# Second cross-attention: queries six places ahead, turned rows and the second half's inverse one place sooner, the last output product behind a feed-forward

## The chip, the cores and the metric

The kernel runs on one core of one Trainium2 chip. A core has a matrix engine (TensorE, PE in the profile), a vector engine (VectorE, DVE), a scalar engine (ScalarE, ACT), a general engine (GpSimd, POOL) and a queue that issues most of the DMA transfers (SyncE, SP). The metric is the device time of one execution in microseconds (us). All data are 32-bit floats.

## The reference, cut to what matters

The reference computes two transformer blocks on x of shape (8, 512, 256): eight images of 512 rows. Each block has self-attention, cross-attention to a short context and a feed-forward. The change lies in the second block's cross-attention and in the start of its feed-forward:

```python
cross_in = _adaln(x, cond, ln1_w, ln1_b, g1_w, g1_b, b1_w, b1_b)
ctx_n = _ln(context, ca_lnc_w, ca_lnc_b)
x = _attn(cross_in, ctx_n, ca_wq, ca_wkv, ca_wo, ca_bo) + x   # 16 heads of 64, 64 context rows
ffn_in = _adaln(x, cond, ln2_w, ln2_b, g2_w, g2_b, b2_w, b2_b)
h = jax.nn.gelu(ffn_in @ ff_w1 + ff_b1, approximate=False)
x = h @ ff_w2 + ff_b2 + x
```

`_attn` projects queries, keys and values, rotates queries and keys by position (rope), takes the softmax of their products and multiplies the result with the values and with `wo`.

## The kernel before

The kernel is one program of stages. The first block's stages and the second block's self-attention take up to about 1829 us of the profile. Then `cross()` does the second cross-attention of all eight images, and after it `feed_forward()` does the second feed-forward, image by image. In these stages the instructions of TensorE, VectorE, ScalarE and GpSimd run in the order in which the Python code issues them (a manual schedule). The order of SP's DMA queue is chosen by a planner, which may move a transfer ahead of another that is not ready by its own estimate. [...]

`cross()` runs a loop of eight places j = 0 to 7 for each image b. An image has 8 pairs of heads, and one place issues one query projection. The pieces are these.

- `queries(n)` projects one eighth of an image's queries (two matmuls of 128x512, recorded as four), and VectorE multiplies the result with the cosines and sines (L853, L854). Two successive n form one group: after the odd one, GpSimd makes the two turned query tiles by a subtraction and an addition (L858, L859). It runs LEAD places ahead, into eight query buffers; the products lie in five `t` buffers.
- `turn(b)` transposes the normalised rows of image b on TensorE (L429), and ScalarE evacuates them with scale and shift (L430) into `hT`, which the queries read.
- `score(b, half)` multiplies the queries of half the heads with the keys; ScalarE takes the exponentials (L1280) into `p`.
- `sums(b, half)` sums `p` over the context on TensorE. ScalarE copies the sums into the single `den` buffer (L1290), two DMAs write them to DRAM (L1293), and one DMA reads them back spread over 128 partitions into `rec` (L1295).
- `inverse(b, half)` takes the reciprocal of `rec` on VectorE (L1300), writes it to DRAM (L1302), and eight DMAs read it back, spread over partitions, into the four `rb` buffers (L1307).
- `scaled(b, half)` multiplies the four 512-column pieces of `p` of that half with `rb`, by turns on GpSimd and VectorE (L1314).
- `outer(b, pp)` multiplies the values of the context with the output weights, once for each image, into `vw` (evacuated by ScalarE, L1251).
- `cross_out(b, t)` makes output tile t: eight matmuls over all pieces of `p`, the first half's four ahead of the second half's, added to x by VectorE (L466).
- `rows_(i, n)` is one of three pieces of the layer norm of a later image (VectorE, and GpSimd for the root and for adding a bias row); `load_kb` and `load_vb` load the next images' keys and values (L963, L968).

Four PSUM banks go round among all users of `bank_x()`. A bank is taken again at the fourth call after it and must have been evacuated by then. The scores have two double banks of their own.

In a place the order is: sums, scores, turn, queries, outer, scaled, inverse, cross_out, loads, rows. An image's second half is only worked off in the next image's places: `sums(b-1, 1)` in place 0, `inverse(b-1, 1)` in place 2, `scaled(b-1, 1)` in place 4, `cross_out(b-1, ...)` in places 5, 6 and 7. For the first half they are `sums(b, 0)` in place 4, `inverse(b, 0)` in place 6 and `scaled(b, 0)` in place 0 of the next image.

`feed_forward()` issues for each image four `up` steps (matmuls into the score banks, Gelu on ScalarE, L1342), a `turn` for the next image, and four `down` steps (matmuls, addition to x, store to the output, L1350). In image 0 the last cross-attention's remaining steps lie between: the last `scaled`, `inverse` and `scaled` after the `up` steps 0, 1 and 2, and the last `cross_out` of four tiles.

Of the kernel before, what the change touches and what calls it, by code (L numbers as in the profile page):

```python
# [17 lines left out]
B, N, D, H, T, CD, FF = 8, 512, 256, 16, 64, 192, 1024  # L18
# [69 lines left out]
def fast_path(ctx: ExitStack, tc: tile.TileContext, a: dict, out: bass.AP):  # L88
# [56 lines left out]
    def row(name):  # L145
        lo, hi = _ROWS[name]
        return rows[:, lo:hi]
# [285 lines left out]
    def normed_in_pieces(pool, b, eps, take):  # L433

        def rows_():
            z = pool.tile([P, NT, D], F32, tag="z", name="z", bufs=1)
            take(z)
            return z

        return norm_pieces(rows_, xs[b], eps)  # L440
# [7 lines left out]
    def add_row(b, r):  # L448

        nc.gpsimd.tensor_tensor(xs[b], xs[b], r[:, None, :].to_broadcast([P, NT, D]), ALU.add)  # L450
# [511 lines left out]
    def load_kb(b):  # L962
        nc.sync.dma_start(kvs[b % 2][0], k_d[:, :, :, b, :].rearrange("p g e t -> p (g e) t"))  # L963

    def load_vb(b):
        for e in range(2):
            r = slice(64 * e, 64 * e + 64)
            nc.sync.dma_start(kvs[b % 2][1][r, :, e, :], v_d[r, :, b, :])  # L968
# [13 lines left out]
    with tc.tile_pool(name="ph4", bufs=2) as wk:  # L982
# [160 lines left out]
        for b, (score, value, sums, inverse, scaled, out_tiles, _) in enumerate(todo):  # L1143
            base = 2 * NG * b
            for g in range(NG):
                if b == B - 1 and g == NG - 1:
                    break
                n = base + 2 * g + 2
# [65 lines left out]
    with tc.tile_pool(name="ph5", bufs=2) as wk:  # L1214
# [9 lines left out]
        def rows_(i, n=None):  # L1224

            if i < 2 * B:
                b = i % B
                if not n and i not in pieces:
                    pieces[i] = normed_in_pieces(nk, b, EPS1, lambda z: turned_rows.update({i: z}))
                for piece in pieces[i] if n is None else pieces[i][n : n + 1]:  # L1230
                    piece()
                if n in (None, 2):
                    add_row(b, row("ffb2" if i // B else "cabo"))

        def turn(i):
            if i < 2 * B:
                am, bm = ((a1, b1), (a2, b2))[i // B]
                turned_rows[i] = transposed((nk, wk)[i % 2], turned_rows[i], i % B, am, bm, 1)
# [3 lines left out]
        def outer(b, pp):  # L1242

            s = ss[b]
            if pp == 0:
                s["vw"] = wk.tile([P, NPAIR, D], F32, tag="vw", name="vw")
            ps = bank_x()
            for i in range(2):
                p = 2 * pp + i
                mm(ps[:, i * D : (i + 1) * D], kvs[b % 2][1][:, p, :, :].rearrange("p e k -> p (e k)"), w_co[:, p, :])  # L1250
            nc.scalar.copy(s["vw"][:, 2 * pp : 2 * pp + 2, :], ps.rearrange("p (i d) -> p i d", i=2))  # L1251

        def queries(n):
            b, m = divmod(n, NPAIR)
            if b == B:
                return
            g, e = divmod(m, 2)
            ps = bank_x()
            for k in range(2):
                mm(ps, w_cq[:, k, m * P : (m + 1) * P], turned_rows[b][:, k, :], k == 0, k == 1)  # L1260

            def dst():
                ss[b][g] = [wk.tile([P, N], F32, tag="q", name="q", bufs=8) for _ in range(2)]
                return ss[b][g]

            rope_half(wk, ss[b], g, e, ps[:, None, :], rope_c[:, None, :], rope_s[:, None, :], [P, 1, N], 5, dst)

        def score(b, half):
            s = ss[b]
            pss = [bank_s() for _ in range(2)]  # L1270
            for e in range(2):
                for j in range(4):
                    r = slice(32 * j, 32 * j + 32)
                    for i in range(2):
                        g = 2 * half + i
                        mm(pss[j // 2][64 * i : 64 * i + 64, j % 2, :], kvs[b % 2][0][r, 2 * g + e, :], s[g][e][r, :],
                           e == 0, e == 1)
            for u in range(2):
                s["p", 2 * half + u] = pr = wk.tile([P, 2, N], F32, tag="p", name="p", bufs=8)
                nc.scalar.activation(pr, pss[u], AF.Exp, scale=HD1 ** -0.5)  # L1280

        def sums(b, half):

            s = ss[b]
            d = bank_x()
            for j in range(4):
                p = 4 * half + j
                mm(d[32 * j : 32 * j + 32, :], sel0, s["p", p // 2][:, p % 2, :])
            den = wk.tile([P, N], F32, tag="den", name="den", bufs=1)
            nc.scalar.copy(den, d)  # L1290
            dd = dram.tile([4, 2, N], F32, tag="den5", name="den5")
            for e in range(2):
                nc.sync.dma_start(dd[:, e, :], den.rearrange("(j r) n -> j r n", j=4)[:, e, :])  # L1293
            s["rec", half] = rec = wk.tile([P, 8 * N // P], F32, tag="rec", name="rec")
            nc.sync.dma_start(rec, flat(dd))  # L1295
# [13 lines left out]
        def scaled(b, half):  # L1309
            s = ss[b]  # L1310
            for j in range(4):
                p = 4 * half + j
                pr = s["p", p // 2][:, p % 2, :]
                (nc.gpsimd, nc.vector)[p % 2].tensor_tensor(pr, pr, s["rb", j], ALU.mult)  # L1314

        def out_tile(b, t, lhsT, w):
            s = ss[b]

            if t % 2 == 0 or b == B - 1 and w is w_f2 and t > 1:
                s["ps"] = bank_x()  # L1320
            project_tile(s["ps"], t % 2, lhsT, w, 8, t)
            if b == B - 1 and w is w_f2 and t > 1:
                x = xs[b][:, t, :]
                nc.vector.tensor_tensor(x, s["ps"][:, (t % 2) * D : (t % 2 + 1) * D], x, ALU.add)
            elif t % 2:
                add_to(b)(t // 2, s["ps"].rearrange("p (j d) -> p j d", j=2))

        def cross_out(b, t):
            out_tile(b, t, lambda k: ss[b]["p", k // 2][:, k % 2, :], ss[b]["vw"])
# [40 lines left out]
            return good  # L1370

        def cross():
            LEAD = 5
            for n in range(LEAD):
                queries(n)
                if n:
                    outer(0, n - 1)
            nc.gpsimd.memset(kvs[1][1], 0.0)
            for b in range(B):
                for j in range(NPAIR):  # L1380
                    if j == 0 and b:
                        sums(b - 1, 1)
                    if j == 4:
                        sums(b, 0)
                    if j % 4 == 0:
                        score(b, j // 4)
                    if j == 2:
                        turn(b + 1)
                    queries(NPAIR * b + j + LEAD)
                    if b and j < 2:  # L1390
                        for pp in (2 * j, 2 * j + 1):
                            outer(b, pp)
                    if b:
                        if j == 0:
                            scaled(b - 1, 0)
                        if j == 2:
                            inverse(b - 1, 1)
                        if j == 4:
                            scaled(b - 1, 1)
                        if j > 4:  # L1400
                            for t in ((0,), (1,), (2, 3))[j - 5]:
                                cross_out(b - 1, t)
                    if j == 2 and b + 1 < B:
                        load_kb(b + 1)
                        load_vb(b + 1)
                    if j > 4:
                        rows_(b + 2, j - 5)
                    if j == 6:
                        inverse(b, 0)
            sums(B - 1, 1)  # L1410

        def feed_forward():
            good = top = None
            for b in range(B):
                for ff in range(4):
                    up(b, ff)
                    if b == 0 and ff < 3:
                        (lambda: scaled(B - 1, 0), lambda: inverse(B - 1, 1), lambda: scaled(B - 1, 1))[ff]()
                if b == 0:
                    for t in range(4):  # L1420
                        cross_out(B - 1, t)
                turn(B + b + 1)
                for t in range(4):
                    down(b, t)
                    if t == 1:
                        rows_(B + b + 2)
                if b == 1:
                    top = extremes()
                if b == 2:
                    good = within(top)  # L1430
            return good

        with tc.manual_schedule(engines={ENG.PE, ENG.DVE, ENG.Activation, ENG.Pool}):
            cross()
            return feed_forward()
# [862 lines left out]
```

## Time and profile before

| What | us |
|---|---|
| Median of 3 runs (lowest to highest) | 2396.58 (2392.86 to 2398.16) |
| Profiled execution, its own time | 2397.98 |
| Its span, from the first to the last instruction | 2396.4 |
| Mean granted TensorE clock | 0.994 |
| First score of the second cross-attention starts | 1828.81 |
| Its images 1 to 7 start at | 1849.08, 1894.57, 1938.18, 1980.10, 2023.61, 2065.53, 2108.99 |
| Its last sums | 2148.56 |
| First `up` of the feed-forward | 2149.56 |

A line of the timeline has the start in us, the duration in us, the engine, the line of the kernel, the operation, what it writes and reads, and how many instructions it merges; in brackets stands the idle time ahead of it on its engine and what ended it. A matmul of 32-bit floats is recorded as two. SPq is the issue of a DMA on the SP queue, not the transfer. In a line of the windows come the window, its length, the busy time (and instructions) of PE, weight loads, DVE, ACT and POOL, then the granted TensorE clock, the DMA engines' busy share and GB/s.

### The profile page before, as it was taken

Reading aid. Unit: us, or ns where it says so; the run is one execution under the profiler, and the core shown is the slowest. Engines: PE = TensorE matmul, PEld = TensorE weight load, DVE = VectorE, ACT = ScalarE, POOL = GpSimd, SP = SyncE. Lnnn points to the kernel's source line nnn. Section 1 sums busy time; section 2 is a strip of 40 time slices with the busy share of each in tenths; the row PEclk is TensorE's granted clock in tenths of the full one; section 3 lists DMA queues with packets and bytes.
Section 4 is the critical chain, followed back from the end, with each engine's and each line's share of the span. In section 5 each row is a group of like instructions: output and inputs, shape, how many; then the busy total and the mean of one; then the engine's idle time right before and its main releaser. Section 6 shows DMA issues by size and latency. Waiting matters only on the chain.

```text
span 2396.4 us, 29139 instructions
## 1 busy us (share of the span) xinstructions
PE 2356.0 (98%) x11348; PEld 1146.4 (48%) x11348; DVE 1079.1 (45%) x2043; ACT 885.4 (37%) x1118; POOL 953.4 (40%) x582
## 2 busy tenths in 40 slices
PE   9999999999999999999999999999999999999998
PEld 4333544544545633434343434343445555557666
DVE  4454544544445345454545455554444444431110
ACT  4665545545542134243434333333342212111221
POOL 4563223323210046464645555555544444431110
PEclk9999999999999999999999999999999999999999
DMA  5120000000003000000101000000123212110000
GB/s 185 37 103 12 16 15 13 17 14 6 12 11 97 0 1 28 14 24 10 28 10 28 10 28 10 26 12 20 44 68 99 68 57 67 60 56 31 18 21 21
DMA packets 84307, 83.85 MB, mean 35 GB/s; under 512 B 42192, under 2 KB 59328, under 8 KB 84160
## 3 DMA queue, kind: packets, MB, share of 16 engines
q1 hardware_dynamic: 82680, 78.73, 10.9%
q8 instruction: 91, 1.49, 0.3%
q0 software_dynamic: 576, 2.10, 0.2%
q10 hardware_dynamic: 904, 1.07, 0.1%
q14 instruction: 56, 0.46, 0.1%
HBM read 71.83 MB, written 10.04 MB: 34 GB/s over the span
## 4 chain that ended last, share of the span: by engine, by line
PE 94%; issue 2%; POOL 1%; DMA 1%; DVE 1%; ACT 1%; SPq 1%; POOLq 0%; ACTq 0%; DVEq 0%
PE ps_X L118 39%; PE ps_S L118 23%; PE ps_D L118 16%; PE ps_O L118 14%; PE ps_X L429 1%; DMA rb<-rec 1%; POOL p L1314 1%; PE ps_X L616 1%; SPq L1307 0%; PE ps_X L576 0%; ACT p L596 0%; DMA rec<-rec 0%; PE ps_D L616 0%; POOL var L567 0%; PE ps_D L429 0%
## 5 line engine op out<-in xcount | busy, mean ns | idle before, releaser
L118 PE MATMUL ps_S<-q,k 32*128 32x512 f32 (+1 forms) x3072 | 416.4, 622 | 2.5 <-ACT p L596 1.5
L1037 ACT ACTIVATE p<-ps_S 128x1024 f32<-128x1024 f32 x256 | 248.4, 1021 | 449.5 <-PE ps_S L118 449.2
L596 ACT ACTIVATE p<-ps_S 128x1024 f32<-128x1024 f32 x256 | 248.2, 1022 | 197.7 <-PE ps_S L118 197.0
L1056 DVE TENSOR_TENSOR sm<-sm,p 128x1024 f32<-128x1024 f32 x128 | 251.4, 2022 | 0.2 <-ACT p L1037 0.2
L118 PEld LDWEIGHTS ps_S<-q,k 32*128 32x128 f32 (+1 forms) x3072 | 141.6, 183 | 228.0 <-issue 161.5
L1019 POOL TENSOR_TENSOR q<-t 128x512 f32<-128x512 f32 x32 | 59.7, 1866 | 328.1 <-DVE t L1017 287.0
L184 POOL TENSOR_TENSOR rstd<-rstd,mhalf 128x4 f32<-128x4 f32 x49 | 50.1, 1023 | 344.4 <-DVE rstd L183 343.8
L1016 DVE TENSOR_TENSOR t<-ps_X,rope_c 128x512 f32<-128x512 f32 x126 | 86.9, 690 | 211.9 <-PE ps_X L118 211.8
L567 POOL TENSOR_TENSOR var<-var,mhalf 128x32 f32<-128x32 f32 (+1 forms) x17 | 87.4, 5141 | 173.7 <-DVE var L561 170.3
L1052 POOL TENSOR_TENSOR sm<-p 128x1024 f32<-128x1024 f32 x64 | 150.0, 2370 | 1.9 <-ACT p L1037 1.9
L118 PE MATMUL ps_X<-hT,w 128*128 128x512 f32 x328 | 150.4, 597 | 0.0
L1102 POOL TENSOR_TENSOR oT<-oT,rb 128x512 f32<-128x512 f32 x63 | 125.2, 2007 | 30.5 <-DMA rb<-rec_d 26.6
L118 PE MATMUL ps_O<-p,v 128*64 128x512 f32 x512 | 134.9, 605 | 0.0
L118 PE MATMUL ps_D<-p,v 128*64 128x512 f32 x512 | 131.6, 592 | 0.0
L118 PE MATMUL ps_O<-p,h 128*32 128x512 f32 x1024 | 130.4, 610 | 0.8 <-ACT p L596 0.8
L118 PE MATMUL ps_X<-w_sa_wv,hT 128*128 128x512 f32 x256 | 118.3, 605 | 0.0
L118 PE MATMUL ps_X<-hT,w_sa_wq 128*128 128x512 f32 x256 | 115.9, 595 | 0.0
L118 PE MATMUL ps_X<-w_sa_wo,oT 128*128 128x256 f32 x512 | 113.9, 381 | 0.6 <-DVE t L1017 0.5
L118 PE MATMUL ps_X<-hT,w_sa_wk 128*128 128x512 f32 x248 | 113.2, 599 | 0.0
L118 PE MATMUL ps_S<-hT,w_ff_w 128*128 128x512 f32 x256 | 111.3, 593 | 0.0
L466 DVE TENSOR_TENSOR x<-ps_X,x 128x512 f32<-128x512 f32 x27 | 18.7, 691 | 198.1 <-PE ps_X L118 198.1
L118 PEld LDWEIGHTS ps_X<-w_sa_wo,oT 128*128 128x128 f32 x512 | 96.1, 190 | 22.8 <-issue 5.3
(282 smaller groups left out, 3543.3 us busy)
## 6 DMA issues: line engine op xcount, KB each, us to landing
rb<-rec SPq DMA_DIRECT2D x128, 128.0 KB
rb<-rec_d SPq DMA_DIRECT2D x124, 128.0 KB
rb<-rec SPq DMA_DIRECT2D x16, 256.0 KB
out_dram<-x SPq DMA_DIRECT2D x15, 256.0 KB
x<-in_x_dram SPq DMA_DIRECT2D x7, 512.0 KB
gate<-modd SPq DMA_DIRECT2D x24, 128.0 KB
k_d<-q POOLq DMA_DIRECT2D x4, 512.0 KB, 3.2
v_d<-v SPq DMA_DIRECT2D x8, 256.0 KB
```

The costliest lines, as they stand in the source:

```text
L118: nc.tensor.matmul(o, lhsT, rhs, start=start, stop=stop)
L184: nc.gpsimd.tensor_tensor(r[:, :n], r[:, :n], mhalf[:, :n], ALU.pow)
L429: nc.tensor.transpose(ps[:, t * P : (t + 1) * P], z[:, t, k * P : (k + 1) * P], ident)
L567: nc.gpsimd.tensor_tensor(var, var, half, ALU.pow)
L596: nc.scalar.activation(pr[u], pss[u], AF.Exp, scale=HD0 ** -0.5)
L616: nc.tensor.transpose(ps[:, t * P : (t + 1) * P], s["oT", g][:, t * P : (t + 1) * P], ident)
L1016: nc.vector.tensor_tensor(c, ps, rope_c, ALU.mult)
L1019: nc.gpsimd.tensor_tensor(r[0], ec, os, ALU.subtract)
L1037: nc.scalar.activation(pr, pss[u], AF.Exp, scale=HD1 ** -0.5)
L1052: nc.gpsimd.tensor_tensor(sm, s["p", g, 0, u], s["p", g, 1, u], ALU.add)
L1056: nc.vector.tensor_tensor(s["sm", g, u], s["sm", g, u], s["p", g, t, u], ALU.add)
L1102: eng.tensor_tensor(o, o, s["rb", g, u], ALU.mult)
```

## The change

The queries run six places ahead of the loop in place of five. The call of `turn` for the next image and the call of `inverse` for the previous image's second half move from place 2 to place 1. In the feed-forward, the last image's `cross_out` moves from ahead of `turn` and `down` of image 0 to behind them. The condition at `outer` keeps its four calls ahead of the loop.

```diff
         def cross():
-            LEAD = 5
+            LEAD = 6
             for n in range(LEAD):
                 queries(n)
-                if n:
+                if 0 < n < 5:
                     outer(0, n - 1)
...
                     if j % 4 == 0:
                         score(b, j // 4)
-                    if j == 2:
+                    if j == 1:
                         turn(b + 1)
                     queries(NPAIR * b + j + LEAD)
...
                         if j == 0:
                             scaled(b - 1, 0)
-                        if j == 2:
+                        if j == 1:
                             inverse(b - 1, 1)
                         if j == 4:
                             scaled(b - 1, 1)
...
                         (lambda: scaled(B - 1, 0), lambda: inverse(B - 1, 1), lambda: scaled(B - 1, 1))[ff]()
-                if b == 0:
-                    for t in range(4):
-                        cross_out(B - 1, t)
                 turn(B + b + 1)
                 for t in range(4):
                     down(b, t)
                     if t == 1:
                         rows_(B + b + 2)
+                if b == 0:
+                    for t in range(4):
+                        cross_out(B - 1, t)
```

## The prediction

> **What bounds the kernel now.** I read the page first: TensorE is busy nearly always, so only its gaps, and stretches where it runs slowly, can be won.
>
> ```profile
> PE 2356.0 (98%) x11348; PEld 1146.4 (48%) x11348; DVE 1079.1 (45%) x2043; ACT 885.4 (37%) x1118; POOL 953.4 (40%) x582
> ```
>
> Second, what TensorE waited for (us in total, times, longest). Five of the seventeen rows belong to the stage that changes:
>
> ```profile
> PE ps_O L118 <- POOL p L1314: 8.3, 6, 2.2
> PE ps_X L118 <- POOL p L1314: 7.8, 5, 2.2
> PE ps_D L118 <- POOL p L1314: 3.8, 2, 2.3
> PE ps_O L429 <- DVE t L854: 1.9, 1, 1.9
> ...
> PE ps_S L118 <- POOL q L858: 0.8, 1, 0.8
> ```
>
> They sum to 22.6 us, 19.9 of it for L1314, `scaled`: `cross_out` at place 5 wants weights that POOL has not yet multiplied. Third, TensorE's timeline; the sums of place 0 mark where an image begins:
>
> ```profile
> 1938.18 1.07 PE L118 MATMUL ps_O<-p,sel 128*32 128x512 f32 x8
> ...
> 1980.10 1.06 PE L118 MATMUL ps_X<-p,sel 128*32 128x512 f32 x8
> ...
> 2023.61 1.06 PE L118 MATMUL ps_O<-p,sel 128*32 128x512 f32 x8
> ```
>
> An image takes 41.9 or 43.5 us in turn. The same view shows image 1 starting at 1849.08, 2 at 1894.57, 7 at 2108.99, and the stage's last sums at 2148.56. Fourth, all engines over places 2 to 5 of image 5:
>
> ```profile
> 2037.50 0.34 DVE L1300 RECIPROCAL rec<-rec 128x32 f32<-128x32 f32 x1
> ...
> 2037.87 0.33 SPq L1302 DMA_DIRECT2D rec<-rec  x1
> ...
> 2038.89 2.51 PE L118 MATMUL ps_S<-q,kb 32*64 32x512 f32 x32
> ...
> 2039.69 0.54 SPq L1293 DMA_DIRECT2D den<-den  x1
> ...
> 2040.32 5.70 SPq L1307 DMA_DIRECT2D rb<-rec  x8
> ...
> 2044.79 1.27 POOL L858 TENSOR_TENSOR q<-t 128x512 f32<-128x512 f32 x1 [4.55 <-DVE t L854]
> 2044.87 1.89 PE L118 MATMUL ps_X<-vw,p 128*128 128x256 f32 x8
> ...
> 2046.01 1.71 POOL L859 TENSOR_TENSOR q<-t 128x512 f32<-128x512 f32 x1
> ...
> 2047.68 2.94 POOL L1314 TENSOR_TENSOR p<-p,rb 128x512 f32<-128x512 f32 x2
> 2048.42 1.07 DVE L1314 TENSOR_TENSOR p<-p,rb 128x512 f32<-128x512 f32 x1 [1.82 <-DMA rb<-rec]
> ...
> 2049.00 1.13 PE L118 MATMUL ps_X<-vw,p 128*128 128x256 f32 x4 [2.23 <-POOL p L1314]
> ```
>
> Two chains meet. The inverse is taken in place 2, its row read back by eight copies only from 2040.32 (SP stands 1.2 us at a den write that waits for ACT), and the last lands near 2048.4. And POOL, in order, first turns place 4's query (L858, L859), then scales. Either alone would make `cross_out` late. Fifth, the clock in windows after such stalls:
>
> ```profile
> 1920.00:1923.00 3.00, 2.45 (x7) 1.81 (x8) 2.53 (x7) 0.00 (x0) 1.58 (x1) 0.78 0.04 6
> 1923.00:1926.00 3.00, 3.00 (x6) 1.39 (x5) 0.00 (x0) 0.00 (x0) 0.00 (x0) 0.65 0.00 0
> ...
> 2134.00:2138.00 4.00, 3.73 (x9) 3.01 (x10) 1.62 (x5) 0.00 (x0) 0.22 (x1) 0.50 0.00 0
> ```
>
> The number before the DMA share is the granted clock: 0.65 to 0.78 in image 2, 0.50 in image 7. That is the 1.6 us by which even images are longer than odd ones.
>
> [...] gaps of 2.2 plus 0.55 us cost clock in some images and not in others. [...]
>
> **The change part by part.** TensorE's own work is unchanged: per image 2 sums at 1.0, 2 scores at 1.9, 8 queries at 1.72 to 1.82 (14.0), 4 outer products at 0.86, turned rows 0.87, 4 output tiles at 3.45: 38.1 us, 38.2 with edges. Image 3's 41.9 less its idle 2.8, its long score 0.5 and slow first matmuls 0.2 gives 38.4, so the sum holds.
>
> *Lead 6.* One query goes ahead of the loop (+1.72) and one leaves image 7 (-1.72). Odd queries, those with POOL's turning, now fall on places 1, 3, 5, 7 instead of 0, 2, 4, 6. So POOL is free before both `scaled`: 2.5 to 3.0 us (L858 and L859) go from ahead of each. The second score of an image, 2.51 against 1.97 us for the first, waits on L859 of place 2; that query is now a place sooner: -0.54 each.
>
> *Inverse in place 1.* From the start of an image's sums: den is written at +1.9, rec requested at +4.1 (2027.70), landed by +5.8 (a request-to-reciprocal of 1.65 us is seen at 2152.80 to 2154.44). In place 1 TensorE reaches the end of turn and query at +9.0; VectorE's two rope products end at +10.4; the reciprocal at +10.7, where it was +13.9 to 14.2. Row write, 1.45 us to the copies (2017.14 to 2018.61): +12.2 to +17.2; 3.0 us to landing as now: last row +20.2. POOL's second product ends near +20, VectorE's at +20.9. `cross_out` wants them from +22.4: a margin of 1.5 to 2.5 us. Next image's vb load (two issues, 1.25 us, 256 KB) gets ready at +10.7 beside it: bounded at 0 (it fits in the 1.45 us) to 1.5 us, taken as 0.5; the margin covers it. The four rb buffers must be free: POOL's first-half products end near +7.
>
> *Turn in place 1.* 0.87 us of TensorE moves one query ahead; its two banks were freed by sums and query of place 0. The next image's first query then has 3.4 us of other matmuls as cover for ACT's two 0.78 us evacuations, against 1.7 before. Nothing; a loss of at most 1 us if a bank were late.
>
> *Last output product.* 13.8 us go from before to behind turn and `down(0)`. There is no gap there now (2149.56 to 2191.9 is solid); the last scaled row is done at 2164.35, wanted at 2166.4. `down(0)` wants the last gelu (2164.86) at about 2167.3. Nothing; later images run up, turn, down with no gap. The move pays only if the last scaled chain gets later.
>
> The sum: images 2 to 6, 2108.99 - 1894.57 = 214.4 less 5 x 38.2 = **23.4**. Image 1: 45.5 less 38.2 is 7.3; image 0's short places leave its first-half rows as late as now, so scaled(0,0) still holds VectorE's ropes; I leave 1.0: **6.3**. Image 0: its second score, **0.5**. Image 7: 39.6 less 29.5 of work (three queries) is 10.1 of stall and slow clock. After, places 2 and 3 are empty on TensorE, so `cross_out` wants rows at +15.9 while they land at +15.9 to +20: idle 3.2 plus slow clock 2.0 (2 to 8 in all): **4.9**. Together 35.1: the span 2396.4 becomes 2361.3, the execution 2397.98 becomes 2362.9; the median of runs lies 1.4 below that execution, so 2361.5.
>
> **The rivals.** *The copies still stand behind the den write.* SP's queue is ordered by the planner. With den 1.6 us after the reciprocal it put den first; with 8 us (half 0) it put the copies first; now there are about 5. If den goes first, rows land as late as now; only POOL's earlier start, the score and some clock are won: 1.5 to 2 us in each of six images, 3 to 4 in image 1, 2 to 3 in 7: about 17, so 2380.
>
> *Transfers are the limit anyway*: another wait takes the place of L1314's (a bank, a DMA window fuller than its present 0.5 to 0.67 during the copies), and all but the scores' 4 us come back: 2393. Against it: DMA's mean over an image is 0.2.
>
> *Slower.* The reciprocal in place 1 waits for rec, on VectorE, in order; behind it stand the ropes of query 2, whose bank query 5 of the image takes again at +19. TensorE feels it only if the reciprocal runs after +17.5, that is if rec lands 11.7 us later than now, say behind the vb load and the copies on SP; to eat 5 us per image it must be past +22. Then 2410. The 4.6 us of slack between +5.8 and +10.4 speaks against it.
>
> **How the numbers follow.** Forecast 0.72 (2354 to 2369), copies behind den 0.18 (2370 to 2384), another wait 0.05, slower 0.05. 2354 is every stall gone; up to 2379 takes in half of the second case, about 8 in 10. Faster 0.92, within 0.2% (4.8 us, about what these runs can tell) 0.03, slower 0.05.
>
> **What would show it.** Right: images 2 to 6 each 38 to 38.5 us; no L1314 wait of TensorE but in images 1 and 7; second scores at 1.97; L1314 on POOL without L858 and L859 just ahead in place 4; copies' issue 1.5 us after the row write; clock 1.0 in images 2 to 6. Wrong: a den write between row write and copies in SP's queue; a VectorE wait on rec at L1300; a TensorE wait on a bank (DVE t L854) in each image.

## The result and the profile after

The changed kernel takes 2362.12 us (median of 4 runs, 2357.97 to 2368.43) against 2397.37 us (2392.86 to 2399.95) before; the ratio on record is 0.9857 with a 95% interval of 0.983 to 0.9884. The prediction was 2361.5. The execution in the profile is the shortest of the four, 2357.97 us with a span of 2356.2.

The page of the changed kernel, its first line of engines:

```profile
PE 2336.6 (99%) x11348; PEld 1140.2 (48%) x11348; DVE 1073.4 (46%) x2043; ACT 885.2 (38%) x1118; POOL 945.0 (40%) x582
```

TensorE's busy time fell by 19.4 us and its idle time by 20.8 us (the span less the busy time: 40.4 before, 19.6 now). Busy time fell although the number of matmuls is the same, because the records count slow matmuls as busy (before, image 2 has 40.83 us of busy time for 202 records at a mean granted clock of 0.96, image 3 39.13 us for 202 at 1.00), and long second scores too (2.51 us before, 1.97 now). What TensorE waited for in the stage (us in total, times, longest) is reduced to two rows:

```profile
PE ps_D L118 <- POOL p L1314: 3.2, 2, 2.2
...
PE ps_D L118 <- DVE p L1314: 0.3, 1, 0.3
```

All three waits are in image 7. The rows for L854 and L858 are gone, and the 19.9 us for L1314 on POOL are 3.2. TensorE's timeline shows the images' starts, at the sums of place 0:

```profile
1923.85 1.07 PE L118 MATMUL ps_X<-p,sel 128*32 128x512 f32 x8
...
1961.92 1.06 PE L118 MATMUL ps_D<-p,sel 128*32 128x512 f32 x8
...
1999.98 1.07 PE L118 MATMUL ps_X<-p,sel 128*32 128x512 f32 x8
...
2038.05 1.06 PE L118 MATMUL ps_D<-p,sel 128*32 128x512 f32 x8
```

Images 3, 4 and 5 take 38.07, 38.06 and 38.07 us, where before images took 41.9 and 43.5 in turn. The alternation has gone with the waits. The timeline of image 5, all engines, for the same instructions as before:

```profile
2010.43 0.34 DVE L1300 RECIPROCAL rec<-rec 128x32 f32<-128x32 f32 x1
...
2010.80 0.33 SPq L1302 DMA_DIRECT2D rec<-rec  x1
...
2012.57 5.04 SPq L1307 DMA_DIRECT2D rb<-rec  x8
...
2015.27 1.97 PE L118 MATMUL ps_S<-q,kb 32*64 32x512 f32 x32
...
2017.04 1.28 POOL L859 TENSOR_TENSOR q<-t 128x512 f32<-128x512 f32 x1
...
2017.71 1.10 SPq L1293 DMA_DIRECT2D den<-den  x2
2018.26 2.52 POOL L1314 TENSOR_TENSOR p<-p,rb 128x512 f32<-128x512 f32 x2
...
2020.40 1.52 DVE L1314 TENSOR_TENSOR p<-p,rb 128x512 f32<-128x512 f32 x2
2020.71 3.62 PE L118 MATMUL ps_D<-vw,p 128*128 128x256 f32 x16
```

Counted from the image's start at 1999.98, the reciprocal is at +10.4 us, the eight copies go out at +12.6, now ahead of the den writes, and the last product ends at +21.9. `cross_out`, at +20.7, runs its eight matmuls (sixteen records) without a gap: its first piece of the second half is wanted 1.7 us after its start, at +22.4. The second score takes 1.97 us. L859 directly ahead of POOL's products is the turning of place 3's query. It ends in time. Before, the turning of place 4's query stood there, and it did not.

Windows of the changed kernel (window, length, busy time and count of PE, weight loads, DVE, ACT, POOL, then granted clock, DMA share and GB/s), over image 4 and image 7:

```profile
1961.92:1999.98 38.06, 38.06 (x201) 23.48 (x200) 19.41 (x41) 8.74 (x12) 18.83 (x14) 1.00 0.24 70
2076.12:2108.85 32.73, 29.21 (x178) 18.87 (x177) 11.66 (x29) 8.74 (x12) 10.87 (x8) 1.00 0.19 59
```

Image 4 has no idle time on TensorE. Image 7 still waits 3.5 us.

From here on "the stage" is a length in the profiled execution of each kernel, from the start of the first score to the last sums, plus 1.72 us for each query that was added ahead of it. That is 319.8 us before and 281.0 + 1.7 = 282.8 in the changed kernel: 37.0 us less. The profiled spans differ by 40.2. Of the remainder 2.7 us lie ahead of the stage, where nothing changed, and about 0.5 after it. One execution of each kernel was profiled, and the stage itself is not quite the same each time: two more executions that run the same code up to the last sums (the second profile of the changed kernel, and the experiment that moves only the last output product back) have 0.4 and 2.7 us more, 2.3 of the 2.7 in image 7. A difference of less than about 3 us in one stage length is therefore weak evidence. Images 2 to 6 are firmer: each repeats to 0.01 us.

### The profile page after: what moved, and what is told of

It reads as the page before. It is cut to its first block, busy times and chain, and to the rows that moved or that the text cites. A ratio compares the mean times of both kernels' runs of the same rounds, so it can differ in the third digit from the quotient of the medians.

```text
span 2356.2 us, 29152 instructions
## 1 busy us (share of the span) xinstructions
PE 2336.6 (99%) x11348; PEld 1140.2 (48%) x11348; DVE 1073.4 (46%) x2043; ACT 885.2 (38%) x1118; POOL 945.0 (40%) x582
## 4 chain that ended last, share of the span: by engine, by line
PE 96%; DMA 1%; DVE 1%; ACT 1%; issue 1%; POOL 0%; SPq 0%; ACTq 0%; DVEq 0%; POOLq 0%
PE ps_X L118 40%; PE ps_S L118 24%; PE ps_D L118 16%; PE ps_O L118 14%; PE ps_X L429 1%; DMA rb<-rec 1%; PE ps_X L616 1%; PE ps_X L576 0%; ACT p L596 0%; PE ps_D L616 0%; PE ps_D L429 0%; POOL var L567 0%; DMA rec<-rec 0%; PE ps_D L576 0%; ACT den L1072 0%
## 5 line engine op out<-in xcount | busy, mean ns | idle before, releaser
L1342 ACT ACTIVATE hid<-ps_S,cols 128x512 f32<-128x512 f32 x64 | 40.5, 684 | 176.3 <-PE ps_S L118 176.3
```

The source lines that it names most:

```text
L1342: nc.scalar.activation(s["hid"][:, f, :], ps[:, i, :], AF.Gelu, bias=col("ffb1")[:, f : f + 1])
```

## The experiments

The theory was that two chains made `cross_out` late, POOL's order and the late inverse, and that either alone would keep it late. The rivals were that only the late inverse and its transfers counted, or that the mere depth of the lead did.

**Lead and turned rows alone.** The kernel before, with these edits:

```diff
-            LEAD = 5
+            LEAD = 6
...
-                if n:
+                if 0 < n < 5:
...
-                    if j == 2:
+                    if j == 1:
                         turn(b + 1)
```

> Kernel before plus lead 6 and the turned rows in place 1; the inverse stays in place 2, the last output product where it was. Two chains (mine): POOL is free before the products, but the inverse is taken at +14.3 us of an image, its copies go out behind a den write at about +16.6, the last row lands near +24.6, so TensorE still waits some 1.8 us an image, now more for the third row on POOL and the last on VectorE; second scores fall from 2.51 to 1.97. An image takes about 40 us, the time is about 2376. Late transfers alone (rival): the copies are as late as before, so only the scores are won, 4 us: 2393. Lead alone (rival): nearly all is won here, 2363.

Measured: 2369.72 us (2368.72 to 2370.4), ratio 0.9883 (0.9867 to 0.99); the stage is 293.3 us, 26.4 less than before. The timeline of image 4:

```profile
1983.46 0.33 SPq L1302 DMA_DIRECT2D rec<-rec  x1
...
1985.28 0.54 SPq L1293 DMA_DIRECT2D den<-den  x1
1985.93 4.93 SPq L1307 DMA_DIRECT2D rb<-rec  x8
...
1989.63 1.27 POOL L1314 TENSOR_TENSOR p<-p,rb 128x512 f32<-128x512 f32 x1 [2.05 <-DMA rb<-rec]
...
1992.20 1.26 POOL L1314 TENSOR_TENSOR p<-p,rb 128x512 f32<-128x512 f32 x1 [1.30 <-DMA rb<-rec]
...
1993.52 0.70 PE L118 MATMUL ps_X<-vw,p 128*128 128x256 f32 x2 [0.83 <-POOL p L1314]
```

The copies stand behind a den write as before and go out 2.47 us after the row write (2.45 us in image 5 before), and POOL now stands idle for them, 2.05 and 1.30 us, instead of turning a query. In images 1 to 6 TensorE waits 0.8 to 1.2 us an image, where I expected 1.8, and the time is 6 us below the 2376 expected. Images 2 to 6 take 39.4 to 39.9 us. So most of the gain comes from here, but not all, which speaks against the two rivals in their pure form.

**Inverse alone.** The kernel before with

```diff
-                        if j == 2:
+                        if j == 1:
                             inverse(b - 1, 1)
```

> Kernel before plus only the inverse in place 1. Two chains (mine): rows land by about +19.5 us, but POOL still turns the query of place 4 ahead of its first product and ends it near +24.9, wanted at +23: a wait of about 1.9 and 0.4 us stays in each image and second scores stay at 2.51; 4 to 12 us are won over the stage, about 2388. Late transfers alone (rival): nearly all but the scores is won, 2367. Lead alone (rival): nothing, 2397.

Measured: 2388.69 us (2383.89 to 2393.09), ratio 0.9966 (0.9951 to 0.9981); the stage is 309.3 us, 10.4 less. The timeline of image 4:

```profile
1999.59 1.58 POOL L858 TENSOR_TENSOR q<-t 128x512 f32<-128x512 f32 x1 [4.55 <-DVE t L854]
...
2001.14 1.71 POOL L859 TENSOR_TENSOR q<-t 128x512 f32<-128x512 f32 x1
...
2002.82 2.49 POOL L1314 TENSOR_TENSOR p<-p,rb 128x512 f32<-128x512 f32 x2
...
2004.13 2.39 PE L118 MATMUL ps_O<-vw,p 128*128 128x256 f32 x6 [2.56 <-POOL p L1314]
```

The rows are there, since both products run back to back without a wait for a DMA, but POOL turns the query of place 4 first. TensorE still waits 2.56 us, in each of images 1 to 6. The 2388 came out, but not from where I expected it. The stage by images shows this (us; in brackets the gain, with the 1.72 us of the moved query in image 7):

| Kernel | Image 0 | Image 1 | Images 2 to 6 | Image 7 | Stage |
|---|---|---|---|---|---|
| Before | 20.3 | 45.5 | 214.4 | 39.6 | 319.8 |
| Lead and turned rows | 19.8 (0.5) | 39.5 (6.0) | 198.4 (16.0) | 35.6 (4.0) | 293.3 (26.4) |
| Inverse | 20.3 (0.0) | 43.3 (2.2) | 214.0 (0.4) | 31.7 (7.9) | 309.3 (10.4) |
| Both (changed kernel) | 19.8 (0.5) | 38.2 (7.3) | 190.3 (24.1) | 34.5 (5.1) | 282.8 (37.0) |

In images 2 to 6 an early inverse alone is worth nothing that can be told (0.4 us) while POOL's order stands, and about 8 us on top of the lead: of the 24.1 us there, 7.6 need both. Nearly all of the 10.4 us comes from images 1 and 7. Image 7 has no query left for POOL to turn in place 4, and with lead 5 a query still covers place 2; there the early rows suffice, and no wait on L1314 is left. That the two gains add up to 36.8 us against 37.0 for both is an accident of the whole stage: in images 2 to 6 they add up to too little, in image 7 to too much.

**Lead seven.** Is it the depth, or which places the odd queries fall on? The changed kernel with

```diff
-            LEAD = 6
+            LEAD = 7
...
-                    if j == 1:
+                    if j == 0:
                         turn(b + 1)
```

> The changed kernel with lead 7 (and the turned rows in place 0, which lead 7 needs), so that the odd queries fall on the even places again; inverse in place 1, last output product behind the feed-forward. Two chains, with POOL's order as the cause (mine): POOL has L858 and L859 ahead of its products in place 4 again, TensorE waits 1.5 to 2.5 us an image, second scores stay at 1.97: about 2378. Depth of the lead as the cause (rival): as the changed kernel or better, 2362.

Measured: 2387.14 us (2381.91 to 2394.84), ratio 0.9955 (0.9943 to 0.9968); the stage with two added queries is 310.1 us. One more query of lead gives back 27 of the 37 us. TensorE waits 2.56 us for POOL in each of images 1 to 6, as with the inverse alone, and second scores stay at 1.97. So the depth isn't the cause. The odd queries in places 0 and 4 are. (The turned rows moved too, to place 0, but TensorE never waits for them here.) I had expected 2378: the wait is just above the 1.5 to 2.5 us expected, and what comes on top of it was left too small. An image of 38.07 us plus the wait would be 40.6; the images 2 to 6 take 41.2 to 42.9. Windows of this kernel, at the wait and after it, in image 3 and in image 4:

```profile
1960.50:1963.00 2.50, 2.40 (x9) 1.70 (x10) 0.00 (x0) 0.00 (x0) 1.14 (x1) 1.00 0.02 7
1963.00:1966.00 3.00, 3.00 (x12) 2.01 (x11) 1.29 (x2) 0.00 (x0) 0.00 (x0) 1.00 0.00 0
...
2001.70:2004.30 2.60, 2.50 (x8) 1.82 (x9) 0.00 (x0) 0.00 (x0) 1.15 (x1) 0.82 0.00 0
2004.30:2007.00 2.70, 2.70 (x5) 1.16 (x4) 0.00 (x0) 0.00 (x0) 0.00 (x0) 0.54 0.00 0
```

The same wait of 2.56 us costs no clock in image 3 (41.2 us) and drops it to 0.54 in image 4 (42.9 us).

**POOL's order alone.** The kernel before, lead 5, with the GpSimd products (pieces 0 and 2) issued ahead of the query and VectorE's (1 and 3) where they were:

```diff
+                    if b and j % 4 == 0:
+                        scaled(b - 1, j // 4, (0, 2))
                     queries(NPAIR * b + j + LEAD)
...
-                            scaled(b - 1, 1)
+                            scaled(b - 1, 1, (1, 3))
```

and likewise for `scaled(b - 1, 0)`.

> Kernel before, lead 5, with one change: in places 0 and 4 GpSimd's two products of scaled are issued ahead of the query, so ahead of its turning; VectorE's two stay behind it. Mine, POOL's order carries most of what lead 6 gave: waits on L1314 near 1 us an image, second scores still 2.51, about 2374. Rival, the lead itself gave it: waits stay at 2.8 us an image, 2395.

Measured: 2382.4 us (2380.04 to 2385.15), ratio 0.9933 (0.9919 to 0.9946); the stage is 301.2 us, 18.6 less. The timeline of image 5:

```profile
2028.17 2.50 PE L118 MATMUL ps_S<-q,kb 32*64 32x512 f32 x32
...
2033.57 1.27 POOL L1314 TENSOR_TENSOR p<-p,rb 128x512 f32<-128x512 f32 x1 [4.06 <-DMA rb<-rec]
...
2038.31 1.25 PE L118 MATMUL ps_X<-vw,p 128*128 128x256 f32 x4 [1.41 <-POOL p L1314]
```

Images 2 to 6 take 39.7 to 40.9 us, 40.2 on average, against 42.9 before and 39.7 with the lead. The difference to the lead is that of the second score, 2.50 for 1.97 us. So in these images POOL's order and that score account for what the lead does. The waits and the scores were as expected, and yet 2374 was missed by 8 us; it had no breakdown by images, so where it went wrong is not shown. Against the lead the stage is 7.9 us longer: 3.1 in image 1, which keeps its 1.5 us wait of the turned rows on VectorE (L854), 2.6 in images 2 to 6, 1.8 in image 7 and 0.5 in image 0.

**Turned rows back in place 2.** The changed kernel with

```diff
-                    if j == 1:
+                    if j == 2:
                         turn(b + 1)
```

> The changed kernel with the turned rows back in place 2, right ahead of the first query that reads them. Mine: the move hides the scalar engine's evacuation; without it TensorE waits 0.6 to 0.7 us an image for hT, about 5 us in all: 2367. Rival, the move is free either way: 2362. Rival, the turn set the new period: well over 2370.

Measured: 2366.62 us (2364.47 to 2367.05), ratio 0.9869 (0.9852 to 0.9885); the stage is 289.2 us, 6.4 more than in the changed kernel. The waits of TensorE, and one of them in the timeline:

```profile
PE ps_O L118 <- ACT hT L430: 1.4, 3, 0.5
PE ps_X L118 <- ACT hT L430: 1.4, 3, 0.5
```

```profile
2019.88 1.98 PE L118 MATMUL ps_X<-hT,w_ca_wq 128*128 128x512 f32 x4 [0.48 <-ACT hT L430]
```

In images 2 to 6 the first query of the next image waits 0.48 us for the evacuation, and an image takes 38.8 us for 38.1: 3.7 us in all. Image 1, where the turned rows wait 1.8 us on VectorE, is 2.2 us longer, and image 0 is 0.7. Image 7 is not longer. The move goes with lead 6 and is worth its cover.

**The last output product back ahead of turn and down.** The changed kernel and, beside it, the changed kernel itself once more:

```diff
+                if b == 0:
+                    for t in range(4):
+                        cross_out(B - 1, t)
                 turn(B + b + 1)
                 for t in range(4):
                     down(b, t)
...
-                if b == 0:
-                    for t in range(4):
-                        cross_out(B - 1, t)
```

> The changed kernel itself, run beside the next three so that they share a chip: 2362, images 1 to 6 at 38.1 us each.

> The changed kernel with the last output product back ahead of the turn and the down steps. Mine: the last scaled rows end near 2125.8 us in the changed kernel's profile and would be wanted at 2125.4 to 2127, so at most 0.5 us is lost and the time is the changed kernel's, within 1 us. Rival, the move covers a wait: 2 us or more slower than the changed kernel, with a TensorE wait on L1314 after the last sums.

Measured: the changed kernel 2363.77 us (2360.05 to 2365.64), 0.9851 (0.9836 to 0.9866); with the product ahead 2364.2 us (2362.05 to 2367.29), 0.9859 (0.9844 to 0.9874). No difference. The timeline with the product ahead:

```profile
2128.98 7.07 PE L118 MATMUL ps_X<-vw,p 128*128 128x256 f32 x32
...
2129.96 1.26 POOL L1314 TENSOR_TENSOR p<-p,rb 128x512 f32<-128x512 f32 x1 [2.91 <-DMA rb<-rec]
...
2130.56 1.22 DVE L1314 TENSOR_TENSOR p<-p,rb 128x512 f32<-128x512 f32 x1 [2.11 <-ACT hid L1342]
```

The first output tile wants POOL's piece 2.6 us after its start, at 2131.6, and has it at 2131.2; it wants VectorE's at 2132.0 and has it at 2131.8. From the last sums to the end of the span the two profiles take 246.8 us (product ahead) and 246.7. So the move buys nothing here, and the rows are in time without it by a margin of 0.2 to 0.4 us.

**Covering image 7.** What is left is image 7, where places 2 and 3 are empty on TensorE. Two `up` steps of the feed-forward's image 0 were moved there, in place 5 ahead of `cross_out` or in places 2 and 3. The last image's `scaled`, `inverse` and `scaled` then follow the last sums with the remaining `up` steps:

```diff
+                        if b == B - 1 and j == 5:
+                            up(0, 0)
+                            up(0, 1)
...
-                    up(b, ff)
-                    if b == 0 and ff < 3:
-                        (... scaled, inverse, scaled ...)[ff]()
+                    if b or ff > 1:
+                        up(b, ff)
+                    if b == 0 and ff > 0:
+                        (... scaled, inverse, scaled ...)[ff - 1]()
```

For places 2 and 3 the first hunk is `if b == B - 1 and j in (2, 3): up(0, j - 2)`.

> The changed kernel, and in place 5 of image 7 two up steps of the feed-forward's image 0 go ahead of the output product, whose rows are late there; the three remaining steps of the last image follow the last sums one after the other up step. Mine: the 3.5 us of waits on L1314 in image 7 are covered by 6.9 us of matmuls: the stage up to the first down step gets 3.5 to 4.5 us shorter, 2358; the last output product, behind the feed-forward, has the slack for it. Rival, the wait moves to the last scaled rows or to the Gelu's table: no gain, 2362.

> The version with two up steps ahead of the output product in place 5 of image 7, once more, beside the next one: 2357 to 2360.

> The same two up steps in the empty places 2 and 3 of image 7, ahead of the sums and the second score. Mine: the late rows are covered as before, the wait of 1.15 us of the up step on the exponentials goes, and the second score no longer catches POOL's turning; against it stand two more changes of ScalarE's table (1.28 us each) ahead of the exponentials, which nobody waits for soon. From the first score to the first down step 1 to 1.7 us shorter than with place 5. Rival, the second score waits for the Gelu to leave its bank: no gain.

Measured: in place 5, 2357.49 us (2355.33 to 2361.22), 0.9831 (0.9818 to 0.9845), and beside the early version 2355.75 us (2355.07 to 2357.48), 0.9828 (0.9814 to 0.9841). In places 2 and 3, 2356.14 us (2355.78 to 2360.19), 0.9832 (0.9819 to 0.9846). From the first score to the first `down` step the changed kernel takes 296.7 us in its own profile (1827.81 to 2124.55) and 297.2 in its second. Place 5 takes 293.9 and 293.6, places 2 and 3 292.2. The timelines of image 7, place 5 first:

```profile
2094.61 7.13 PE L118 MATMUL ps_S<-hT,w_ff_w 128*128 128x512 f32 x16 [1.15 <-ACT p L1280]
2101.58 7.07 PE L118 MATMUL ps_D<-vw,p 128*128 128x256 f32 x32
```

```profile
2090.22 7.03 PE L118 MATMUL ps_S<-hT,w_ff_w 128*128 128x512 f32 x16
...
2100.49 7.17 PE L118 MATMUL ps_D<-vw,p 128*128 128x256 f32 x32
```

In both, the output product runs without a wait on L1314. In place 5 the `up` step waits 1.15 us for the exponentials to leave its bank, so 2.8 to 3.5 us are won where I expected 3.5 to 4.5; the early version wins that wait back and 4.5 to 4.9 us in all. Its second score stays long, 2.38 us, which I had expected to end. The three medians don't tell the two places apart, but all lie 6 to 8 us under the changed kernel's 2363.77. Only the first of them was measured beside it, and their ranges overlap a little, so the profile's 3 to 5 us are the better figure. These two are the fastest versions I found.

## Why the prediction was right, point by point

**The sum.** Against 35.1 us the stage gave 37.0 in the profiled executions:

| Term | Predicted | Measured |
|---|---|---|
| Images 2 to 6 | 23.4 | 214.4 - 190.3 = 24.1 |
| Image 1 | 6.3 | 45.5 - 38.2 = 7.3 |
| Image 0 | 0.5 | 20.3 - 19.8 = 0.5 |
| Image 7, less the query that left it | 4.9 | 39.6 - 32.7 - 1.7 = 5.1 |

An image's own work, put at 38.2 us, measured 38.07. The microsecond that I left in image 1 for ropes held up on VectorE wasn't lost: its turned rows come ahead of the query whose ropes are late. It is close, though: in other executions of the same code image 1 took up to 38.55 us, with waits of 0.2 to 0.3 us on L854.

That the median came out 0.6 us from 2361.5 is luck: four runs scatter over 10 us, the second set of runs gave 2363.77, and the stage gave 1.9 us more than the sum. The term of image 7 is luck too, within its range: in the other two executions the image took 33.2 and 35.1 us for 32.7, which makes the gain 4.6 and 2.8 us for 5.1. The five images that carry two thirds of the sum repeat in the changed kernel, and are not luck.

Three slips in the working changed nothing. Six of the seventeen rows of waits belong to the stage, since the 0.4 us on VectorE's L1314 lies in image 7. The terms of TensorE's own work add up to 37.9, not 38.1. The rival of the den write counts six images where images 2 to 6 are five.

**The chain of the inverse** was right in its order and late by up to 1 us at its end: in image 5 the reciprocal is at +10.4 (predicted +10.7), the copies at +12.6 (+12.2), POOL's second product ends at +20.8 (+20) and VectorE's at +21.9 (+20.9). The vb load between the row write and the copies is not free. Where neither it nor a den write lies between, the copies follow the row write after 1.45 to 1.48 us; with it after 1.74 to 1.80 us in images 1, 2, 3 and 5, and after 3.50 us in image 4:

```profile
1972.73 0.33 SPq L1302 DMA_DIRECT2D rec<-rec  x1
1973.15 1.25 SPq L968 DMA_DIRECT2D kv<-v_d  x2
1976.23 4.94 SPq L1307 DMA_DIRECT2D rb<-rec  x8
...
1982.34 1.80 POOL L1314 TENSOR_TENSOR p<-p,rb 128x512 f32<-128x512 f32 x1 [0.86 <-DMA rb<-rec]
```

That is 2.0 us late, more than the bound of 1.5 that I had set. In image 4 POOL does wait for a row, and its product ends at +22.2, wanted at +23.3; about 1 us of margin is left. Image 4 is late with the inverse alone and with lead seven too, at 3.33 and 3.18 us after the row write; why this load and not the others, the traces don't show.

The planner put the copies ahead of the den writes in images 1 to 6. In image 7, where the distance is short, it put a den write between. SP's queue there and TensorE's waits:

```profile
2086.93 0.32 SPq L1302 DMA_DIRECT2D rec<-rec  x1
2088.82 0.50 SPq L1293 DMA_DIRECT2D den<-den  x1
2089.42 4.97 SPq L1307 DMA_DIRECT2D rb<-rec  x8
```

```profile
2094.55 1.25 PE L118 MATMUL ps_D<-vw,p 128*128 128x256 f32 x4 [2.15 <-POOL p L1314]
2096.83 0.70 PE L118 MATMUL ps_D<-vw,p 128*128 128x256 f32 x2 [1.03 <-POOL p L1314]
2097.86 4.15 PE L118 MATMUL ps_D<-vw,p 128*128 128x256 f32 x18 [0.33 <-DVE p L1314]
```

That is 3.5 us of idle time where 3.2 were put. The slow clock beside it, 2.0 us by my estimate, is not there in this execution: the granted clock of image 7 is 1.00 in its window above, and its 29.2 us of busy time are only 1.4 more than its own work of 27.8, 0.5 of them the long second score. In one of the other two it was 0.95 (33.2 us); in the other (35.1 us) twenty records of the output product took 7.33 us, where eighteen take 4.15 us above. So this term differs from run to run.

**POOL free before both `scaled`** was the right cause, but one sign that I gave for it was wrong. I wrote that L858 and L859 would not stand just ahead of the products in place 4. They do: they are the turning of place 3's query and end at +18.3, so POOL and not the rows opens the products in image 5. It is early enough by a whole place. The margin was smaller than the 1.5 to 2.5 us that I gave: I counted from +22.4, when the first piece of the second half is wanted, and by that count 0.5 us were left in image 5. The wait stayed away because the last piece is wanted only with the last of the eight matmuls, at +23.7, so that product had 1.8 us.

**"Either alone would make `cross_out` late"** holds in images 2 to 6, but I gave no weights, and they are unequal: with the late inverse alone left, an image takes 39.7 us for 38.1; with POOL's order alone left, 42.8, where it was 42.9 before. In image 7, where no query is left to turn in place 4, it does not hold: the early inverse alone takes all waits on L1314 away. There lead 6 costs something: image 7 takes 34.5 us with the moved query, against 31.7 with the inverse alone.

**The turned rows and the last output product** were put at nothing, and cost nothing. The first is worth 6.4 us of the stage if it is left out while the rest is made, because with lead 6 the cover of place 2 is gone. I had named the cover without pricing its loss in the prediction.

**The rivals.** For the second half, the copies stand behind a den write in image 7 alone; for the first half they do so once, in image 0. No reciprocal of images 1 to 7 waited for rec: L1300 waited once, 0.4 us, in the last chain behind the last sums. No bank made TensorE wait in this execution.

## What to carry to other kernels

When an engine that runs in order serves two pieces of work, ask which one stands first in the place where the other is urgent. Shifting a software pipeline by one step can change that by parity, and a further step in the same direction can undo it, as lead 7 did. A wait behind two chains that end close together needs both removed; measure each alone, and compare image by image, since the gains of a whole stage can add up by accident. A stall on TensorE is to be priced with the slow matmuls that may follow (with lead seven, 1.7 us more in image 4 than in image 3 for the same wait of 2.56 us). Where a stage runs out of work to cover a wait, as image 7 does, work of the next stage whose inputs are already there can fill it.

## What the runs showed of the hardware that I had not expected

The clock after a stall isn't a fixed price: the same 2.56 us of waiting, ahead of the same matmuls, left the clock at 1.00 in one image and took it to 0.82 and 0.54 in the next, 1.7 us of difference between the two images (41.2 and 42.9 us). The gap alone doesn't decide it, and what does is not shown.

Two profiled executions of the changed kernel reached the first score of the stage at 1827.81 and at 1834.30 us, with the stage itself equal to 0.4 us. Their spans differ by 6.2 us, so between these two the difference is made ahead of the stage. That is why lengths of stages tell more here than times of runs, though the stage has its own scatter in images 1 and 7.
